# A decoder layer on one core: the order of cross-attention's products, the feed-forward's banks and the last block's transposes

## The chip, the core and the metric

The kernel runs on one core of a Trainium2 chip. A core has five engines that work side by side: TensorE (in the profile PE, its weight loads PEld), VectorE (DVE), ScalarE (ACT), GpSimd (POOL) and SyncE (SP), which here issues most of the DMAs. TensorE writes to PSUM[...]. The metric is the device time of one execution in microseconds; lower is better.

## What is computed

One layer of a decoder on 2048 tokens (32 sequences of 64) with 512 features, all in fp32. Three sublayers follow one another, each with a residual addition and a layer normalization behind it:

```python
x = layernorm(x + attention(x))                # 32 heads, 512 cached keys and 64 new ones
x = layernorm(x + cross_attention(x, context)) # 32 query heads on 8 key/value heads, 64 keys
z = x @ W.T + b                                # feed-forward
m = sum_e p[e] * (x @ A[e]) @ B[e]             # 8 terms of rank 16
gamma = minimum(0.5 * norm(z) / (norm(m) + 1e-6), 1)
x = layernorm(x + z + gamma * m)
```

## The kernel before

The tokens are cut into four blocks (`tb`) of 512, each of four tiles of 128. The large products (queries, keys and values, output projections) are computed by a scheme with seven products of half the size in each dimension in place of eight; a product is called by its number, 1 to 7, and its operands are sums that GpSimd makes ahead (`token_sums`, `output_sums`, `left_sums`, `right_sums`). One product is four matmuls of 128x128 by 256 columns. The seven are collected in three PSUM banks: x takes products 1 and 2, y takes 6, 7 and 4, z takes 5 and 3. After every product VectorE (for queries in part ScalarE) reads the bank and adds it into the result, and the next product into the same bank must wait for that read.

Self-attention fills the first two thirds of the time, and the change leaves it as it is. Then keys and values for cross-attention are computed for all groups and kept in DRAM.

**Cross-attention** runs over 32 units, one per key/value head `g` and block `tb`, `tb` innermost. The loop (lines 1274 to 1343) works on two units at once: it makes the queries and scores of unit `n` and finishes unit `n - 1`. For TensorE, VectorE and GpSimd the program's order is the order in which they run, up to unit 31, from where VectorE is ordered by the scheduler. ScalarE's and SyncE's order is the scheduler's throughout. The pieces of a turn are:

- `queries(n)` and its steps 1, 6, 5, 7, 2, 4, 3: the query products (qx in the profile), read by lines 313 to 337.
- `attend(n - 1)`: the values (pox, line 1139), eight matmuls of 64 rows, two side by side, from transposed weights `pTx` that DMAs have put in place. ScalarE (line 1157) and VectorE (line 1159) move the result to `oTx`, and GpSimd makes four sums of it (`output_sums`, lines 266 to 269).
- `scores(n)`: sx, line 1068, 32 small matmuls with 64 columns for each pair of tiles, two side by side.
- `largest`, `exponentials`, `denominators`, `weights`, `turn`: the softmax of unit `n` on VectorE and ScalarE, and its 32x32 transposes; `move(n)` issues eight DMAs from SyncE that complete the transposition into `pTx`.
- `project(n - 1, ...)`, called by `steps`: the output products (wx) of unit `n - 1`, read by lines 361 and 369.

The order before is: queries 1, 6, 5, 7, 2, 4, then pox, query 3, wx 1, sx, and wx 6, 5, 2, 7, 3, 4 with softmax parts between them. Query and wx banks and half of pox come from one pool of four banks (`xps`), the other half of pox from `xpo` (two banks), sx from `xsc` (two banks).

**Feed-forward** (lines 1193 to 1231) runs for a block at a time: block 0 at the end of unit 31's turn, block 1 between pox and the wx products of unit 31, blocks 2 and 3 after the loop. It makes pu (a rank-128 product), scales it to uT on VectorE, and for each of four tiles pz (four matmuls) and pm (one, from uT), all in banks of `xps`. VectorE adds the bias (z), ScalarE sums the squares of z and m, GpSimd adds z into the tile `acc`, VectorE computes gamma, adds gamma times m and normalizes (`layernorm_tile`, lines 174 to 184); SyncE sends the tile out. Before a block's feed-forward, `transpose_block` (x2, line 129) transposes its normalized tokens into `x1T`: four groups of transposes, each into a bank of `xps` that ScalarE or VectorE copies out (line 131). For the last block these stand between the feed-forwards of blocks 2 and 3.

Of the kernel before, what the change touches and what calls it, by code (L numbers as in the profile page):

```python
# [9 lines left out]
F32 = mybir.dt.float32  # L10
# [6 lines left out]
P = 128  # L17
# [35 lines left out]
def decoder_layer(  # L53
# [40 lines left out]
    make_identity(nc, ident)  # L94
    bk = const.tile([P, NKV], F32, name="bk")
# [23 lines left out]
    def bank(shape, name, tag=None):  # L119
        if tag in special:  # L120
            v = special[tag]
            return v.rearrange("p (a b) -> p a b", a=shape[1])
        return psum[-1].tile(shape, F32, tag=tag or "ps", name=name)
# [50 lines left out]
    def layernorm_tile(tb, j, name):  # L174
        a = acc[tb][:, j, :]
        st = small.tile([P, 6], F32, tag="st", name=f"st_{name}_{tb}_{j}")
        nc.vector.bn_stats(st, a)
        mv = small.tile([P, 2], F32, tag="mv1", name=f"mv_{name}_{tb}_{j}")
        nc.vector.bn_aggr(mv, st)
        rstd = small.tile([P, 1], F32, tag="rstd1", name=f"rstd_{name}_{tb}_{j}")  # L180
        nc.vector.tensor_scalar_add(rstd, mv[:, 1:2], LN_EPS)
        nc.scalar.activation(rstd, rstd, AF.Sqrt)
        nc.vector.reciprocal(rstd, rstd)
        nc.vector.tensor_scalar(a, a, mv[:, 0:1], rstd, ALU.subtract, ALU.mult)
# [76 lines left out]
    def output_sums(o, name):  # L261

        a = {(i, j): o[j][:, :, i * HF : (i + 1) * HF] for i in range(2) for j in range(2)}
        t = {i: big.tile([P, 2, HF], F32, tag=f"so{i}", name=f"{name}_{i}") for i in range(1, 5)}
        sub = ALU.subtract
        nc.gpsimd.tensor_tensor(t[1], a[1, 0], a[1, 1], ALU.add)  # L266
        nc.gpsimd.tensor_tensor(t[2], t[1], a[0, 0], sub)
        nc.gpsimd.tensor_tensor(t[3], a[0, 0], a[1, 0], sub)  # L268
        nc.gpsimd.tensor_tensor(t[4], a[0, 1], t[2], sub)
        return {1: a[0, 0], 2: a[0, 1], 3: t[4], 4: a[1, 1], 5: t[1], 6: t[2], 7: t[3]}  # L270
# [692 lines left out]
    with ExitStack() as ph:  # L963
# [160 lines left out]
        def attend(n):  # L1124
# [35 lines left out]
            left = output_sums(oTs.pop(n), f"sox{g}_{tb}")  # L1160
# [32 lines left out]
        def feed_forward(tb):  # L1193
            wf, af, bm = ffn_w
            pu = bank([P, TB], f"pu{tb}")
# [6 lines left out]
            for i in range(TPB):  # L1202
                u = f"{tb}_{i}"
# [3 lines left out]
                pm = bank([P, DIM], f"pm{u}")  # L1207
                for c in range(NC):
                    if c == 2:
                        nc.tensor.matmul(pm, uT[:, cols], bm, start=True, stop=True)  # L1210
                    nc.tensor.matmul(
                        pz, xT[tb][:, c, cols], wf[:, c, :], start=(c == 0), stop=(c == NC - 1)
                    )
                nrm = small.tile([P, 2], F32, tag="nrm", name=f"nrm{u}")
# [5 lines left out]
                nc.scalar.activation(sqz, z, AF.Square, accum_out=nrm[:, 0:1])  # L1220
                nc.gpsimd.tensor_tensor(a, a, z, ALU.add)
# [4 lines left out]
                nc.vector.tensor_tensor(gam, gam, nrm[:, 0:1], ALU.mult)  # L1226
                nc.vector.tensor_scalar(gam, gam, CLAMP, 1.0, ALU.mult, ALU.min)
# [35 lines left out]
        def parts(n, *made):  # L1263

            for part, pr in made:
                if n < N:
                    part(n, pr)

        def steps(n, *made):
            if n >= 0:  # L1270
                project(n, *made)

        mxs, es, dens, scales = {}, {}, {}, []
        for n in range(N + 1):
# [25 lines left out]
            if n < N:  # L1300
                q.step(4)
                q.read()
            if n > 0:
                attend(n - 1)
            if n < N:
                q.step(3)
                q.read()
                if behind:
                    next_tokens(n + 1, 0)
                next_tokens(n + 1, 1)  # L1310
            if n == N:
                feed_forward(1)
            steps(n - 1, 1)
            if n < N:
                if n + 1 < N:
                    load_kv(n + 1)
                scores(n)
            parts(n, (largest, 0), (largest, 1), (exponentials, 0), (exponentials, 1))
            if n < N and g == 0:
                for j in range(TPB):  # L1320
                    a = acc[tb][:, j, :]
                    nc.gpsimd.tensor_tensor(a, a, bo, ALU.add)
            steps(n - 1, 6)
            parts(n, (denominators, 0), (denominators, 1))
            steps(n - 1, 5)
            parts(n, (weights, 0))
            if n < N and tb == NTB - 1 and g + 1 < NKV:
                load_xq(g + 1)
            steps(n - 1, 2, 7)
            parts(n, (weights, 1))  # L1330
            steps(n - 1, 3)
            parts(n, (turn, 0), (turn, 1))
            if n < N:
                move(n)
            if n > 0:
                steps(n - 1, 4)
                if n < N and tb == 0:
                    if g > 0:
                        load_xo(g)
                    if g == NKV - 1:  # L1340
                        load_ffn()
            if n == N - 1:
                feed_forward(0)
        scales.pop(0)()
        feed_forward(2)
        while later:
            later.pop(0)()
# [50 lines left out]
```

## Time and profile before

| | us |
|---|---|
| median of 3 runs | 3067.01 (3065.17 to 3067.51) |
| the profiled execution | 3067.85 |
| its span, first to last instruction | 3066.1 |
| cross-attention, one unit in the middle | 28.51 |
| feed-forward of block 3, first to last matmul | 20.84 |
| granted TensorE clock, mean | 0.999 |

The profile is of one execution; its times differ a little from the median's. A line of the chain of waits gives the start, the length and what ran. A line of the waits reads: who waited, for whom, total us, how often, the longest. A line of the timeline is start, length, engine, line, operation, out<-in, shapes, and in brackets the idle time before it and what ended it. Matmuls overlap one another, so TensorE's pace is read from start to start.

The last stretches by engine (start:end, length, then busy time and number of instructions of PE, PEld, DVE, ACT, POOL, the granted clock, the DMA share and GB/s):

```profile
2948.57:2969.17 20.60, 20.60 (x50) 9.07 (x48) 15.04 (x41) 9.05 (x24) 3.81 (x3) 1.00 0.15 44
2969.17:2974.61 5.44, 4.32 (x33) 3.02 (x31) 5.20 (x13) 2.90 (x8) 1.27 (x1) 1.00 0.22 79
2974.61:2995.92 21.31, 20.94 (x50) 9.14 (x49) 16.18 (x40) 6.98 (x22) 8.85 (x7) 1.00 0.08 29
2995.92:3008.61 12.69, 12.35 (x57) 10.56 (x56) 11.80 (x26) 1.33 (x5) 1.27 (x1) 1.00 0.16 58
3008.61:3034.33 25.72, 22.86 (x65) 10.73 (x64) 19.51 (x50) 11.02 (x30) 5.07 (x4) 1.00 0.07 28
3034.33:3055.17 20.84, 20.84 (x48) 9.01 (x48) 14.53 (x38) 6.14 (x20) 3.80 (x3) 1.00 0.09 34
```

These are, in order: feed-forward 0; transposes of block 2 with pox of unit 31; feed-forward 1; wx of unit 31; feed-forward 2 with the transposes of block 3; feed-forward 3.

### The profile page before, as it was taken

Reading aid. Unit: us, or ns where it says so; the run is one execution under the profiler, and the core shown is the slowest. Engines: PE = TensorE matmul, PEld = TensorE weight load, DVE = VectorE, ACT = ScalarE, POOL = GpSimd, SP = SyncE. Lnnn points to the kernel's source line nnn. Section 1 sums busy time; section 2 is a strip of 40 time slices with the busy share of each in tenths; the row PEclk is TensorE's granted clock in tenths of the full one; section 3 lists DMA queues with packets and bytes.
Section 4 is the critical chain, followed back from the end, with each engine's and each line's share of the span. In section 5 each row is a group of like instructions: output and inputs, shape, how many; then the busy total and the mean of one; then the engine's idle time right before and its main releaser. Section 6 shows DMA issues by size and latency. Waiting matters only on the chain.

```text
span 3066.1 us, 42299 instructions
## 1 busy us (share of the span) xinstructions
PE 3028.1 (99%) x14944; PEld 2317.9 (76%) x14944; DVE 2171.1 (71%) x3945; ACT 766.4 (25%) x1776; POOL 961.1 (31%) x789
## 2 busy tenths in 40 slices
PE   8999999999999999999999999999999999999998
PEld 6677777777767777777777769988888888888864
DVE  7787787777877877877877764436666656666677
ACT  2323222222322233232222221211111111111232
POOL 4221321321321321322322123036434444444421
PEclk9999999999999999999999999999999999999999
DMA  5444444444344354344344343231121121121101
GB/s 173 128 132 129 109 116 128 107 122 119 104 125 118 102 130 119 101 128 120 101 125 113 91 129 141 99 108 50 55 62 52 52 66 51 51 69 49 49 28 42
DMA packets 201105, 298.66 MB, mean 97 GB/s; under 512 B 44352, under 2 KB 95040, under 8 KB 200896
## 3 DMA queue, kind: packets, MB, share of 16 engines
q1 hardware_dynamic: 186224, 280.60, 33.2%
q10 hardware_dynamic: 12624, 11.16, 1.3%
q0 software_dynamic: 2048, 4.20, 0.5%
q8 instruction: 120, 1.97, 0.3%
q14 instruction: 89, 0.73, 0.1%
HBM read 107.05 MB, written 20.97 MB: 42 GB/s over the span
## 4 chain that ended last, share of the span: by engine, by line
PE 91%; DVE 4%; SPq 2%; DMA 1%; ACT 1%; issue 1%; ACTq 0%; DVEq 0%
PE po L677 15%; PE s L631 14%; PE sx L1068 2%; PE pox L1139 2%; SPq L669 2%; PE wx_2y L292 1%; PE w_0y L292 1%; PE wx_1y L292 1%; PE wx_0y L292 1%; PE w_3y L292 1%; PE qx_3y L292 1%; PE qx_2y L292 1%; PE qx_0y L292 1%; PE q_2y L292 1%; PE wx_3y L292 1%; PE qx_1y L292 1%
## 5 line engine op out<-in xcount | busy, mean ns | idle before, releaser
L639 ACT ACTIVATE p<-s,nmax 128x576 f32<-128x576 f32 x512 | 379.1, 741 | 1244.9 <-DVE nmax L636 1234.8
L631 PE MATMUL s<-kT,qT 128*128 128x288 f32 x2048 | 576.5, 407 | 5.0 <-ACT p L639 4.2
L677 PE MATMUL po<-pT,v 128*128 128x512 f32 (+1 forms) x1280 | 549.0, 602 | 6.4 <-DMA pT<-T 6.0
L631 PEld LDWEIGHTS s<-kT,qT 128*128 128x128 f32 x2048 | 387.2, 190 | 108.0 <-issue 18.7
L636 DVE TENSOR_REDUCE nmax<-s 128x1 f32<-128x576 f32 x512 | 384.1, 750 | 59.2 <-PE s L631 59.2
L657 DVE STREAM_TRANSPOSE T<-p 128x576 f32<-128x576 f32 x512 | 394.2, 770 | 4.9 <-DVE nmax L636 0.5
L677 PEld LDWEIGHTS po<-pT,v 128*128 128x128 f32 (+1 forms) x1280 | 213.3, 189 | 206.5 <-issue 177.8
L649 DVE TENSOR_SCALAR p<-p,den 128x576 f32<-128x576 f32 x512 | 319.9, 625 | 17.9
L648 DVE RECIPROCAL den<-den 128x1 f32<-128x1 f32 x512 | 83.9, 164 | 230.0 <-ACT p L639 219.9
L266 POOL TENSOR_TENSOR so<-oT,oT 128x512 f32<-128x512 f32 x32 | 40.7, 1271 | 553.0 <-ACT oT L700 553.0
L268 POOL TENSOR_TENSOR so<-oT 128x512 f32<-128x512 f32 x32 | 40.6, 1270 | 346.2 <-ACT oT L700 95.7
L1247 POOL TENSOR_TENSOR txx<-x1T 128x512 f32<-128x512 f32 x31 | 39.3, 1267 | 229.9 <-PE qx_3z L292 93.2
L207 POOL TENSOR_TENSOR tx<-xT 128x512 f32<-128x512 f32 x31 | 39.6, 1278 | 206.3 <-PE q_3z L292 65.0
L639 ACT ACTIVATION_READ_ACCUMULATOR p<-s,nmax 128x1 f32 x512 | 98.7, 193 | 0.0
L266 POOL TENSOR_TENSOR sox<-oTx,oTx 128x512 f32<-128x512 f32 x32 | 40.5, 1265 | 181.5 <-DVE oTx L1159 176.0
L1085 ACT ACTIVATE ex<-ex 128x512 f32<-128x512 f32 x64 | 39.3, 630 | 203.2 <-DVE ex L1084 203.2
L1068 PEld LDWEIGHTS sx<-kvx,qTx 128*64 128x64 f32 x2048 | 62.3, 138 | 10.6 <-issue 10.6
L700 ACT COPY oT<-po 128x512 f32<-128x512 f32 x128 | 68.2, 587 | 4.7 <-PE po L677 3.8
L1157 ACT ACTIVATE oTx<-pox,bv 128x256 f32<-128x256 f32 x128 | 52.0, 470 | 66.4 <-PE pox L1139 66.4
L1068 PE MATMUL sx<-kvx,qTx 128*64 128x64 f32 x2048 | 66.7, 224 | 0.0
L1139 PE MATMUL pox<-pTx,kvx 64*128 64x256 f32 x512 | 64.6, 389 | 0.0
L1159 DVE TENSOR_SCALAR oTx<-pox,bv 128x256 f32<-128x256 f32 x128 | 53.6, 479 | 9.9 <-PE pox L1139 9.9
(447 smaller groups left out, 5767.6 us busy)
## 6 DMA issues: line engine op xcount, KB each, us to landing
pT<-T SPq DMA_DIRECT2D x1016, 80.0 KB
pT<-T SPq DMA_DIRECT2D x1008, 64.0 KB
xT<-in_xT SPq DMA_DIRECT2D x31, 1024.0 KB
kvx<-kv SPq DMA_DIRECT2D x32, 512.0 KB
pTx<-Tx SPq DMA_DIRECT2D x256, 64.0 KB
kv<-c SPq DMA_DIRECT2D x30, 512.0 KB
wo<-in_woT SPq DMA_DIRECT2D x32, 256.0 KB
xwq<-in_xwq SPq DMA_DIRECT2D x32, 256.0 KB
```

The source lines that it names most:

```text
L266: nc.gpsimd.tensor_tensor(t[1], a[1, 0], a[1, 1], ALU.add)
L292: nc.tensor.matmul(self.banks[b][:, m, :], self.left[i][:, k, m * P : (m + 1) * P], self.right[i][:, k, :], start=(first and m + k == 0), ...
L631: nc.tensor.matmul(s[:, a, :HALF], qTs[n // REP][:, units[n][2], i * P : (i + 1) * P], kTs[g][:, a * HALF : (a + 1) * HALF], start=True, s ...
L636: nc.vector.tensor_reduce(nmax, s[:, :, :HALF], AX.XY, ALU.max, negate=True)
L639: nc.scalar.activation(p.rearrange("q (a k) -> q a k", a=2), s[:, :, :HALF], AF.Exp, bias=nmax, accum_out=den,)
L648: nc.vector.reciprocal(den, den)
L649: nc.vector.tensor_scalar(p, p, den, None, ALU.mult)
L657: nc.vector.transpose(Ts[n][:, :, i, :], ps_.pop((n, i)).rearrange("q (b k) -> q b k", k=SQ))
L677: nc.tensor.matmul(pos[n].rearrange("d (a q) -> d a q", a=NQD), vs[units[n][0]][rows, v, :], pTs[n // 2][rows, :, chunk, :], skip_group_ch ...
L700: nc.scalar.copy(o[:, i, :].rearrange("d (t a k) -> d a t k", t=TPB, a=NQD), pos.pop(n - 1 + i).rearrange("d (a t k) -> d a t k", a=NQD, t ...
L1068: nc.tensor.matmul(s[b * SEQ : (b + 1) * SEQ, i * REP + h, :], qTs[n][:, h, pr * HF + c0 : pr * HF + c0 + SEQ], kvs[n][:, pr, 0, c0 : c0 + ...
L1139: nc.tensor.matmul(po[pr, b][:, i, :].rearrange("d (h a j) -> d h a j", h=REP, a=2), kvs[n][r, pr, 1, i * HD : (i + 1) * HD], pTs[n][r, :, ...
```

## The change

It has four parts.

1. In a turn of the cross-attention loop all seven query products come first, then pox, sx, and wx in the order 1, 5, 6, 3, 7, 2, 4. The softmax parts are spread among them anew, `turn` and `move` come after wx 4, and GpSimd makes the third and fourth of its sums in the other order, following the order of use.
2. The feed-forward takes pu from the score banks and, from block 1 on, pm from the two banks `po0` and `po1`. In a block's first tile pm comes after pz's four matmuls; in the others after the second, as before.
3. VectorE, not GpSimd, adds z into `acc`. The factor 0.5 of gamma moves into ScalarE's square, so gamma takes three small VectorE instructions in place of four. The epsilon of the layer normalization is given to ScalarE's root as a bias from a constant tile that GpSimd sets at the start, in place of an addition on VectorE.
4. The last block's transposes come ahead of the fourth tile of block 2's feed-forward, in place of behind it.

```diff
+    eps = const.tile([P, 1], F32, name="eps")
+    nc.gpsimd.memset(eps, LN_EPS)
...
-        nc.vector.tensor_scalar_add(rstd, mv[:, 1:2], LN_EPS)
-        nc.scalar.activation(rstd, rstd, AF.Sqrt)
+        nc.scalar.activation(rstd, mv[:, 1:2], AF.Sqrt, bias=eps)
...
-    def output_sums(o, name):
+    def output_sums(o, name, fourth_last=True):
...
-        nc.gpsimd.tensor_tensor(t[3], a[0, 0], a[1, 0], sub)
+        if fourth_last:
+            nc.gpsimd.tensor_tensor(t[3], a[0, 0], a[1, 0], sub)
         nc.gpsimd.tensor_tensor(t[4], a[0, 1], t[2], sub)
+        if not fourth_last:
+            nc.gpsimd.tensor_tensor(t[3], a[0, 0], a[1, 0], sub)
...
-        def feed_forward(tb):
+        def feed_forward(tb, between=None):
             wf, af, bm = ffn_w
-            pu = bank([P, TB], f"pu{tb}")
+            pu = sc.tile([P, TB], F32, tag="sc", name=f"pu{tb}")
...
             for i in range(TPB):
+                if between and i == TPB - 1:
+                    between()
...
-                pm = bank([P, DIM], f"pm{u}")
+                pm = (pp.tile([P, DIM], F32, tag=f"po{i % 2}", name=f"pm{u}") if tb else
+                      bank([P, DIM], f"pm{u}"))
                 for c in range(NC):
-                    if c == 2:
-                        nc.tensor.matmul(pm, uT[:, cols], bm, start=True, stop=True)
                     nc.tensor.matmul(
                         pz, xT[tb][:, c, cols], wf[:, c, :], start=(c == 0), stop=(c == NC - 1)
                     )
+                    if c == (NC - 1 if i == 0 else 1):
+                        nc.tensor.matmul(pm, uT[:, cols], bm, start=True, stop=True)
...
-                nc.scalar.activation(sqz, z, AF.Square, accum_out=nrm[:, 0:1])
-                nc.gpsimd.tensor_tensor(a, a, z, ALU.add)
+                nc.scalar.activation(sqz, z, AF.Square, scale=CLAMP, accum_out=nrm[:, 0:1])
+                nc.vector.tensor_tensor(a, a, z, ALU.add)
...
-                nc.vector.tensor_tensor(gam, gam, nrm[:, 0:1], ALU.mult)
-                nc.vector.tensor_scalar(gam, gam, CLAMP, 1.0, ALU.mult, ALU.min)
+                nc.vector.tensor_scalar(gam, gam, nrm[:, 0:1], 1.0, ALU.mult, ALU.min)
...
             if n < N:
                 q.step(4)
                 q.read()
+                q.step(3)
+                q.read()
             if n > 0:
                 attend(n - 1)
             if n < N:
-                q.step(3)
-                q.read()
+                if n + 1 < N:
+                    load_kv(n + 1)
+                scores(n)
                 if behind:
                     next_tokens(n + 1, 0)
                 next_tokens(n + 1, 1)
             if n == N:
                 feed_forward(1)
-            steps(n - 1, 1)
-            if n < N:
-                if n + 1 < N:
-                    load_kv(n + 1)
-                scores(n)
-            parts(n, (largest, 0), (largest, 1), (exponentials, 0), (exponentials, 1))
+            parts(n, (largest, 0), (largest, 1))
...
+            steps(n - 1, 1, 5)
+            parts(n, (exponentials, 0))
             steps(n - 1, 6)
-            parts(n, (denominators, 0), (denominators, 1))
-            steps(n - 1, 5)
-            parts(n, (weights, 0))
+            parts(n, (exponentials, 1), (denominators, 0))
+            steps(n - 1, 3)
+            parts(n, (denominators, 1))
             if n < N and tb == NTB - 1 and g + 1 < NKV:
                 load_xq(g + 1)
-            steps(n - 1, 2, 7)
+            steps(n - 1, 7)
+            parts(n, (weights, 0))
+            steps(n - 1, 2)
             parts(n, (weights, 1))
-            steps(n - 1, 3)
-            parts(n, (turn, 0), (turn, 1))
-            if n < N:
-                move(n)
             if n > 0:
                 steps(n - 1, 4)
+                parts(n, (turn, 0), (turn, 1))
+                if n < N:
+                    move(n)
...
         scales.pop(0)()
-        feed_forward(2)
-        while later:
-            later.pop(0)()
+        feed_forward(2, later.pop(0))
         feed_forward(3)
```

More of the change, by code (lines that the diff above doesn't have):

```diff
@@ L1159, in attend @@
                             nc.vector.tensor_scalar(dst, src, bias, None, ALU.add)
-            left = output_sums(oTs.pop(n), f"sox{g}_{tb}")
+            left = output_sums(oTs.pop(n), f"sox{g}_{tb}", False)
             pjs[n] = Projection(left, wo_cur[g], tb, f"wx{g}_{tb}", XYZ)
@@ L1341, in decoder_layer @@
                         load_ffn()
+            if n == 0:
+                parts(n, (turn, 0), (turn, 1))
+                move(n)
             if n == N - 1:
```

## The prediction

> **What bounds the kernel now.** I read the page first, then the chain of waits inside one cross-attention unit, then what TensorE waited for, then the stretches of the end and the two engines beside it.
>
> ```profile
> PE 3028.1 (99%) x14944; PEld 2317.9 (76%) x14944; DVE 2171.1 (71%) x3945; ACT 766.4 (25%) x1776; POOL 961.1 (31%) x789
> ```
>
> TensorE is busy 99% of the span, and between 2100 and 2890 us the list of its waits is empty. So the change can only give time where TensorE's own work gets shorter, or at the end of the kernel, where it does wait. The chain in the middle of a unit (start, length, what) shows the first:
>
> ```profile
> 2407.88 1.73 PE qx_1x L292 x8
> 2409.61 1.73 PE qx_1y L292 x8
> 2411.33 1.93 PE pox L1139 x16
> 2413.26 1.92 PE qx_1z L292 x8
> 2415.18 1.73 PE wx_0x L292 x8
> 2416.91 2.02 PE sx L1068 x64
> 2418.93 1.92 PE wx_0y L292 x8
> 2420.85 1.73 PE wx_0z L292 x8
> ```
>
> A product of eight matmul records takes 1.73, but 1.92 directly after pox (64-row tiles) or sx (64-column tiles): 0.19 for coming back to the full array. A unit is 12 x 1.73 + 2 x 1.92 + 1.93 + 2.02 = 28.5. TensorE's waits from 2890 us on:
>
> ```profile
> PE x L129 <- ACT x1T L131: 2.2, 2, 1.1
> PE pu L1197 <- DVE gam L1224: 1.8, 1, 1.8
> PE x L129 <- ACT qTx L328: 1.0, 2, 0.5
> PE x L129 <- DVE x1T L131: 0.6, 2, 0.3
> PE pm L1210 <- DVE uT L1201: 0.4, 1, 0.4
> ```
>
> And what paces VectorE there (timeline, feed-forward of the last block):
>
> ```profile
> 3047.54 1.58 DVE L184 TENSOR_SCALAR acc<-acc,mv_f,rstd_f 128x512 f32<-128x512 f32 x1
> 3047.58 1.26 POOL L1221 TENSOR_TENSOR acc<-acc,z 128x512 f32<-128x512 f32 x1 [3.14 <-DVE rstd_f L183]
> 3062.07 0.55 DVE L184 TENSOR_SCALAR acc<-acc,mv_f,rstd_f 128x512 f32<-128x512 f32 x1
> ```
>
> The same normalization takes 1.58 beside GpSimd's addition and 0.55 alone. The chain shows gam L1224 starting at 3044.11, 3049.13, 3054.05 and 3058.97: VectorE needs 4.92 a tile, TensorE 4.29 (pz L1211 after pz). After TensorE's last matmul (3055.2) another 11 us pass.
>
> [...]
>
> **The change, part by part.** Sums are against the profiled execution: span 3066.1, whole 3067.85 (1.75 around it).
>
> *Pox directly ahead of sx.* The third query product no longer follows pox, so it takes 1.73: 0.19 less per unit. Pox still follows a full-array product (1.93). Sx now follows pox, one entry as before (2.02); the trace has no pox-to-sx pair, so this entry could cost 0.1 less or up to 0.19 more; I take the same, since each is one change of shape. W1 then follows sx (1.92). Units 1 to 31: 31 x 0.19 = **-5.9**.
>
> Does a wait take its place? Put P at the start of pox in the new order: sx at P+1.9, w1 at 3.9, w5 5.8, w6 7.5, w3 9.2, w7 11.0, w2 12.7, w4 14.4.
> - *GpSimd's sums*: before, they start at P+3.1 and need 1.27 each, so t1, t2, t4, t3 are there at 4.4, 5.7, 6.9, 8.2; used at 5.8, 7.5, 9.2, 11.0. More slack than before, where w6 stood at 7.6.
> - *Banks*: products into one bank now stand closer (w5-w3, w6-w7 with one product between), so VectorE must have read the first in 1.7 us. VectorE in its written order: two q3 additions to 1.0, evictions 1.3 to 2.95, both maxima to 4.7, w1's two reads (0.68 and 1.22) 6.0 to 7.8, w5's read to 8.5 (needed at 9.2), exponentials, w6's read to 10.1 (needed 11.0), second exponentials, denominators, w3's read to 12.0, denominators, w7's read to 13.5 (needed 14.4). Slack 0.7 to 0.9.
> - *Transposes and pT*: turn ends at P+18.3, before at 18.4. The eight issues take 4.95 and their packets land about 1.4 later, at P+24.7; the next pox is at P+28.3. In seven units the first quarter of the next group's query weights is now issued ahead of these DMAs and waits for the next unit's first product (P+18.1), plus up to 1.4 for its own issue (5.46 for four): slack falls from 3.6 to about 2.3. Key loads and weights keep their place relative to P; the output weights' last quarter comes 1.9 earlier, and GpSimd's sums queue behind it with at least 5 us over.
>
> All of it is cover, so nothing is added. The first unit is special: pox(0) took 2.36 instead of 1.93, waiting for pT; one product later it finds it landed: **-0.4**. The 1.55 wait for L333 at 2063 stays.
>
> *Head.* The added memset of eps stands on GpSimd before the iota chain (0.1); VectorE waits for the block indices until 3.24 while the iota result is used by 2.27: hidden, 0.
>
> *VectorE's tile in the feed-forward.* Removed: adding eps to the variance (0.2), one gam instruction (0.2), the slow normalization (1.58 to 0.55). Added: z's addition, two SBUF inputs, which the trace does not have in this place; the nearest rows are 0.68 (L1218) and 0.69 (L1094), so a pitch of 0.60 when another instruction follows; between 0.55 and 1.3. ScalarE's root now has nothing of VectorE beside it, 0.45 from aggregate to reciprocal. Sum of pitches: z 0.60, normalization 0.46, addition 0.60, gam 0.65, L1228 0.79, statistics 0.73, aggregate and root 0.45, reciprocal 0.17, some 0.05 of waiting for ScalarE = 4.5. So VectorE remains the slower of the two, at 4.5 against 4.29 (before 4.92).
> - *Last block* from its pu: the first gam comes at the same place (9.7 after pu: now pm last, before z last). Then 2.8 to the next z, two tiles of 4.5, and 5.1 for the last: 16.9, before 3062.62 - 3044.11 = 18.5. **-1.7** with rounding.
> - *Block 0 to block 1*: before, block 0's last z is read 22.0 after its pu; after, 9.7 + 2.8 + 2 x 4.5 = 21.5. That read and the first copy hold the third and fourth transposes (stretch 2969.17 to 2974.61): 0.6 less. Placing pm last in the first tile removes block 1's wait for uT: 0.37 and 0.1 of restart, as behind every stop. **-1.2** with rounding. The wait of 0.34 in the last output products goes, but w3 there waits for VectorE's read of w5, about as long: 0.
>
> *Last transposes ahead of tile 3.* Before: feed-forward 2 takes from 3008.61 to 3029.21 on TensorE, then 5.12 until pu of block 3 (2.14 of transposes, 2.98 of waits: a bank, a bank, copies). After: the transposes stand after tile 2, at 16.3 from its pu. The fourth needs the bank of tile 2's z, which VectorE reads by 17.7, and stands at 17.9. Tile 3's z bank needs the first copy, done by 17.7, needed at 18.4. The copies (0.58 to 0.64 each) delay gam of tile 2 by about 1.2 on VectorE, which tile 3's 4.29 covers. pu of block 3 has a score bank and starts at 22.7, before 25.72: **-3.0**, between -2 (a second wait for a bank) and -3.
>
> Sum: 5.9 + 0.4 + 1.7 + 1.2 + 3.0 = 12.2. 3067.85 - 12.2 = 3055.65 for the profiled execution, which lies 0.84 above the median: **3054.8**.
>
> **Rivals.**
> - *A shape change between two tiled modes costs as much as two.* Then the 5.9 go: 3067.0 - 6.3 = 3060.7. For: no such pair in the trace. [...]
> - *The end gives half.* The addition on VectorE costs 1 us, or the copies make tile 3 late, and the last three terms give 2.9 instead of 5.9: 3057.8. For: VectorE has no slack there. Against: nothing contends any more.
> - *Slower: VectorE late in the output products.* One place: w3 waiting for w5's read, w7 for w6's. It decides when VectorE runs over 0.7 us later than worked out; above 1.1 us late (0.4 x 31 = 12.2) the whole is slower. At 1.4 us: 31 x 0.7 = 21.7 - 12.2 = +9.5, 3076.5. For: it is busy 17.7 of a unit's 28.5 us, and only one product lies between where two or more lay. Against: each of its steps comes from a measured row, and its two-input additions that GpSimd slows (L1094, 0.69 to 1.47) stand behind the reads that decide.
>
> **How the numbers follow.** Forecast 0.68, half the end 0.12, no saving from shapes 0.12, VectorE late 0.08. The range holds the forecast with its open costs (3051 to 3058) and the two faster rivals: 3051 to 3061. About 0.2% (6.1 us) is what a measurement of this kernel can tell from no change; the shape rival lies on that border and is split. Faster 0.84, same 0.08, slower 0.08.
>
> **What would show it.** In the changed profile's chain a unit of 28.3 instead of 28.5, the third query product at 1.73, sx at about 2.0 directly after pox, and no TensorE wait between 2100 and 2880. In the end: L184 at 0.55 everywhere, gam of the last block every 4.5, no wait of pu of block 3. Wrong would be waits of wx z or y for VectorE's L361, sx above 2.2, or pu waiting for copies.

## The result, and the profile after

| | before | after |
|---|---|---|
| median, us | 3067.28 (3065.17 to 3069.44, 6 runs) | 3056.09 (3054.30 to 3057.02, 6 runs) |
| ratio, 95% interval | | 0.9962 (0.9952 to 0.9973) |
| the profiled execution | 3067.85 | 3057.02 |
| its span | 3066.1 | 3055.2 |
| first query product of cross-attention to pu of block 0 | 906.49 | 903.34 |
| pu of block 0 to the end | 117.50 | 109.70 |

The kernel is 11.2 us faster; 3054.8 was forecast. The sum is near, but by luck, for it is made of other parts: the cross-attention loop gave 3.1 instead of 6.3, and the end gave 7.8 instead of 5.9. Distances in a trace are taken here from the first query product of cross-attention, since the start of that product differs from one execution to the next (2039.2 to 2044.8 in the thirteen further traces of this study) for kernels that are the same up to there but for the one memset of eps.

The engines' line of the page after the change shows TensorE at 99%, as before:

```profile
PE 3021.4 (99%) x14944; PEld 2320.5 (76%) x14944; DVE 2171.4 (71%) x3929; ACT 768.5 (25%) x1776; POOL 944.8 (31%) x774
```

The chain of waits inside the same unit (start, length, what):

```profile
2410.10 1.73 PE qx_1z L296 x8
2411.83 1.93 PE pox L1143 x16
2413.75 2.02 PE sx L1072 x64
2415.77 1.92 PE wx_0x L296 x8
```

The third query product takes 1.73, pox 1.93 and sx 2.02: sx costs directly behind pox what it cost behind a product. One product of 1.92 is left. A unit is 28.31 instead of 28.51, in every undisturbed unit. TensorE's waits from 2100 us on:

```profile
PE x L131 <- ACT qTx L332: 1.5, 2, 1.0
PE qx_2y L296 <- DVE rstd_x L165: 1.2, 1, 1.2
PE qx_0y L296 <- POOL xwq L203: 1.2, 1, 1.2
...
PE x L131 <- DVE z L1227: 0.4, 1, 0.4
```

The stops of the end (x1T of ScalarE, pu on gam, pm on uT) are gone (one of 0.6 on x1T of VectorE, as before, is left out here); the 0.4 on z is what is left of the stop at block 2's transposes. But the second and third line are new, and the first was 1.0 before. These three are what the loop did not give, and they go against the forecast's sign "no TensorE wait between 2100 and 2880". The first in time stands at the entry of unit 4, the first unit of group 1 (timeline of GpSimd and TensorE):

```profile
2136.66 4.96 POOL L1330 TENSOR_TENSOR acc<-acc,bo 128x512 f32<-128x512 f32 x4
2141.58 1.72 POOL L201 TENSOR_TENSOR xwq<-xwq,xwq 128x512 f32<-128x512 f32 x1
...
2145.06 1.27 POOL L203 TENSOR_TENSOR xwq<-xwq,xwq 128x512 f32<-128x512 f32 x1
2146.38 1.99 PE L296 MATMUL qx_0y<-txx,xwq 128*128 128x256 f32 x8 [1.18 <-POOL xwq L203]
```

In group 0 alone GpSimd also adds the output bias, four additions that stand ahead of the sums of the next group's query weights. Product 6 needs the third of these sums. Before the change it was done 0.75 us ahead of that product; now pox and all that follows it on GpSimd come one product later, and it is ready 1.2 us too late. The second stands at the entry of unit 30, in the last group, where output product 4 brings the layer norm's statistics with it (timeline of VectorE and TensorE):

```profile
2881.71 0.69 DVE L151 BATCH_NORM_STATS2 st_x<-acc 128x6 f32<-128x512 f32 x1
...
2885.40 1.30 DVE L1108 STREAM_TRANSPOSE Tx<-ex 128x512 f32<-128x512 f32 x2 [0.20 <-issue]
2886.63 0.65 DVE L337 TENSOR_TENSOR qTx<-qx_2y,qTx 128x512 f32<-128x512 f32 x1
2887.43 1.96 PE L296 MATMUL qx_2y<-txx,xwq 128*128 128x256 f32 x8 [1.19 <-DVE rstd_x L165]
```

Statistics and turn keep VectorE from 2881.71 to 2886.63, and only then it reads query product 6, which product 7 waits for, as it goes to the same bank. (The list names rstd_x, the small instruction behind the read.) The third is in unit 31:

```profile
2920.23 2.93 ACT L169 ACTIVATE acc<-acc,shift_x,rstd_x 128x512 f32<-128x512 f32 x4 [1.56 <-DVE shift_x L167]
2923.07 0.81 ACT L332 ACTIVATE qTx<-qx_3x,bq 128x256 f32<-128x256 f32 x2
2923.93 1.12 PE L131 MATMUL x<-ident,acc 128*128 128x128 f32 x8 [1.03 <-ACT qTx L332]
```

ScalarE's scaling follows the statistics, its read of query product 2 follows the scaling, and the transposes wait for the bank of that product. Against the rest of the loop these three cost 1.45, 1.43 and 0.54 us, measured from start to start.

The stretches that answer to those shown of before (transposes with pox, feed-forward 1, wx of unit 31, feed-forward 2 with transposes; feed-forward 0 and 3, with 20.60 and 20.76, are nearly as they were):

```profile
2966.15:2970.50 4.35, 3.96 (x33) 3.11 (x32) 3.92 (x11) 3.00 (x8) 0.00 (x0) 1.00 0.18 63
2970.50:2991.20 20.70, 20.70 (x50) 9.23 (x49) 15.34 (x38) 7.24 (x23) 5.15 (x4) 1.00 0.10 38
2991.20:3003.37 12.17, 12.17 (x57) 10.56 (x56) 10.21 (x22) 1.52 (x5) 0.00 (x0) 1.00 0.12 45
3003.37:3025.72 22.35, 22.35 (x65) 10.82 (x64) 16.52 (x44) 10.30 (x27) 0.00 (x0) 1.00 0.06 24
```

TensorE now is idle only in the first of them. VectorE's tile in the last block (timeline):

```profile
3039.68 0.15 DVE L1233 TENSOR_SCALAR gam<-nrm 128x1 f32<-128x1 f32 x1
3043.04 0.54 DVE L185 TENSOR_SCALAR acc<-acc,mv_f,rstd_f 128x512 f32<-128x512 f32 x1
3044.15 0.15 DVE L1233 TENSOR_SCALAR gam<-nrm 128x1 f32<-128x1 f32 x1
```

The normalization takes 0.54 to 0.55 in all sixteen tiles, and in this block gam comes every 4.47 us.

### The profile page after: what moved, and what is told of

Its sections match the earlier page's. It is cut to its first block, busy times and chain, and to the rows that moved or that the text cites. A ratio compares the mean times of both kernels' runs of the same rounds, so it can differ in the third digit from the quotient of the medians.

```text
span 3055.2 us, 42257 instructions
## 1 busy us (share of the span) xinstructions
PE 3021.4 (99%) x14944; PEld 2320.5 (76%) x14944; DVE 2171.4 (71%) x3929; ACT 768.5 (25%) x1776; POOL 944.8 (31%) x774
## 4 chain that ended last, share of the span: by engine, by line
PE 93%; DVE 3%; DMA 1%; SPq 1%; ACT 1%; issue 1%; POOL 0%; ACTq 0%; DVEq 0%; POOLq 0%
PE po L681 16%; PE s L635 15%; PE sx L1072 2%; PE pox L1143 2%; PE w_2y L296 1%; PE q_3y L296 1%; PE w_0y L296 1%; PE w_3y L296 1%; PE qx_0y L296 1%; PE wx_1y L296 1%; PE wx_0y L296 1%; PE wx_3y L296 1%; PE q_2y L296 1%; PE qx_2y L296 1%; PE qx_1y L296 1%; PE qx_3y L296 1%
```

## The experiments

"Trace" is the distance from the first query product of cross-attention to the end of the span; "against after" is the difference in it to the changed kernel. A ratio is to executions of the kernel before that were measured beside the run.

| run | median (runs) | ratio to before, 95% | trace | against after |
|---|---|---|---|---|
| before | 3067.28 (6) | | 1023.99 | +10.95 |
| after | 3056.09 (6) | 0.9962 (0.9952 to 0.9973) | 1013.04 | |
| E1 loop alone | 3065.13 (13) | 0.9992 (0.9983 to 1.0000) | 1024.28 | +11.24 |
| E2 end alone | 3058.77 (7) | 0.9973 (0.9962 to 0.9984) | 1016.44 | +3.40 |
| E3 bias additions late | 3054.43 (5) | 0.9958 (0.9945 to 0.9972) | 1011.56 | -1.48 |
| E4 turn first | 3056.89 (7) | 0.9968 (0.9957 to 0.9979) | 1014.99 | +1.95 |
| E5 additions, statistics and transposes late | 3050.50 (5) | 0.9944 (0.9931 to 0.9958) | 1007.08 | -5.96 |
| E6 pox and sx apart | 3062.22 (20) | 0.9985 (0.9978 to 0.9991) | 1018.91 | +5.87 |
| E7 z on GpSimd | 3057.92 (6) | 0.9968 (0.9956 to 0.9980) | 1014.37 | +1.33 |
| E8 transposes behind the fourth tile | 3059.05 (9) | 0.9973 (0.9963 to 0.9983) | 1015.11 | +2.07 |
| E9 banks back | 3057.10 (6) | 0.9966 (0.9954 to 0.9978) | 1013.93 | +0.89 |
| E10 transposes late | 3051.94 (5) | 0.9950 (0.9936 to 0.9964) | 1009.93 | -3.11 |
| E11 statistics split | 3056.84 (5) | 0.9966 (0.9952 to 0.9980) | 1016.29 | +3.25 |
| E12 arithmetic back | 3060.09 (13) | 0.9978 (0.9969 to 0.9986) | 1017.45 | +4.41 |

The intervals of the ratios are about 0.2% wide, so single medians do not separate differences of one or two us; the traces do, as long as the granted clock is the same. It was not in E1, E4 and E11, whose last column is too high for that reason.

### E1 and E2: the two halves alone

E1 puts only the new loop (diff part 1) into the kernel before, E2 only the rest.

> The kernel before with the first part of the change alone: the new order of cross-attention's unit and the output sums with the fourth one last. The feed-forward, its banks, the normalisation's epsilon and the last block's transposes are as before. Theory 1 (the order saves 0.198 us in each of 31 units and 0.4 in the first, and gives back 3.4 in three waits inside the loop: 1.45 at the entry of unit 4 on the query weights' sums, 1.43 at the entry of unit 30 behind the statistics, 0.54 in unit 31): the time falls by about 3.0 us, and the list of TensorE's waits has qx_0y on xwq with about 1.2 and qx_2y on rstd_x with about 1.2. Rival 2 (the waits of the last group come from the feed-forward's new banks and issue places, which reach into the last units; the order alone is clean): the time falls by 5.0 to 6.5 us, and qx_2y on rstd_x is not in the list.

> The kernel before with everything but the first part: feed-forward in the attention's banks, z added by VectorE, epsilon in the activation, the last block's transposes ahead of tile 3 of block 2; the order of cross-attention's unit is the old one. Theory 1 (the end's gain of 7.8 us arises behind the last unit and does not lean on the new order): the time falls by about 7.8 us (7.2 to 8.2), with no new wait of TensorE in the loop. Rival 2 (part of the end's gain is an effect of the order, for example product 2 as the last but one of the output products, which removes a wait on bank x): the time falls by 5.5 to 7.0 us only, and the sum of both parts alone falls short of the whole.

E1 reached pu of block 0 at 903.34, as the changed kernel did, 3.15 us earlier than before, with the same three waits. So these belong to the order, not to the feed-forward's banks. But then this execution, 3.8 us above E1's median, lost all of it again. Two of the lines of its waits:

```profile
PE pu L1200 <- DVE gam L1227: 1.8, 1, 1.8
PE wx_3z L295 <- DVE gam L1230: 1.2, 1, 1.2
```

The second is new: in the new order the last unit's output products come to a bank that VectorE, at the pace of the old arithmetic, frees late, and 0.9 us go (E12, with the old arithmetic, has this wait too; E9, with the old banks, has not). The first was there before too, but in this execution the granted clock fell to 0.50 within that stop, at 3031.74, for 6.83 us (stretches: the stop, and pu of block 3; the last three numbers are the granted clock, the DMA share and GB/s):

```profile
3031.01:3032.78 1.77, 0.01 (x1) 0.03 (x1) 1.74 (x5) 0.30 (x2) 0.15 (x1) 0.71 0.27 101
3032.78:3039.32 6.54, 6.54 (x9) 2.84 (x10) 2.92 (x9) 0.20 (x1) 0.00 (x0) 0.56 0.14 53
```

From pu's start to that of pz it took 6.38 us, in the kernel before 3.51. Without that the trace would have shown a gain of some 2.6 us (an estimate), which agrees with the medians (2.4, with an interval that reaches down to no gain). E2 gave 7.55 in the trace and had no new wait in the loop, so rival 2's 5.5 to 7.0 fell. Its last clause came true in the traces: both halves together give 10.95, about 0.8 more than the 2.6 and 7.55 of the halves, since the end's new arithmetic removes the wait on wx_3z that the order brings. By the medians the halves add up to the whole (2.4 + 8.8 and 11.2), but these cannot tell 0.8.

### E3: the bias additions behind the weights' sums

```diff
-            if n < N and g == 0:
+            if n < N and g == 0 and tb < NTB - 1:
                 for j in range(TPB):
...
                 load_xq(g + 1)
+            if n < N and g == 0 and tb == NTB - 1:
+                for j in range(TPB):
+                    a = acc[tb][:, j, :]
+                    nc.gpsimd.tensor_tensor(a, a, bo, ALU.add)
```

> The changed kernel with one edit: in the last unit of group 0 GpSimd makes the sums of the next group's query weights ahead of the four additions of the output bias (4.96 us) and not behind them. Theory 1 (these additions hold the sums back, and query product 6 of unit 4 waits 1.18 us for them): the wait of qx_0y on xwq is gone, the start of every later unit is 1.2 to 1.45 us earlier, and the time is 1.2 to 1.5 us under the changed kernel's. Rival 2 (the weights' sums wait for the DMA of the weights or for product 3 of unit 3, not for GpSimd): the sums start where they did, at most 0.3 us earlier, and nothing is gained.

Timeline of GpSimd:

```profile
2135.78 1.27 POOL L201 TENSOR_TENSOR xwq<-xwq,xwq 128x512 f32<-128x512 f32 x1
2141.05 5.87 POOL L1342 TENSOR_TENSOR acc<-acc,bo 128x512 f32<-128x512 f32 x4
```

The sums start 5 us earlier against unit 4's products and wait for nothing; the list of TensorE's waits between 2100 and 2885 is empty, and everything from unit 4 on is 1.45 earlier. Theory 1 holds.

### E4: turn ahead of output product 4 in the last group

```diff
-                steps(n - 1, 4)
+                last = units[n - 1][0] == NKV - 1
+                if not last:
+                    steps(n - 1, 4)
                 parts(n, (turn, 0), (turn, 1))
                 if n < N:
                     move(n)
+                if last:
+                    steps(n - 1, 4)
```

> The changed kernel with one edit: in the last group the turn and its DMAs stand ahead of output product 4's read and the statistics that hang on it, as in the kernel before; everything else of the new order stays. Theory 1 (VectorE has no gap there: turn 1.24 us and statistics 3.6 us fill it from the weights to the read of query product 6 in either order, and the softmax stands about 1 us nearer to the next unit's products than before; only the gap of 0.3 us ahead of output product 4's read is won): qx_2y still waits, 0.7 to 1.0 us instead of 1.19, and the time is 0.2 to 0.8 us under the changed kernel's. Rival 2 (the turn behind the statistics is the whole cause): the wait of qx_2y is gone and that of the transposes on qTx is back at 1.0 in total, and the time is 1.7 to 2.0 us under the changed kernel's.

```profile
PE x L131 <- ACT qTx L332: 2.7, 2, 2.2
PE qx_2y L296 <- DVE rstd_x L165: 0.6, 1, 0.6
```

The list of TensorE's waits shows the wait of unit 30 halved, to 0.6 where theory 1 had 0.7 to 1.0, but in unit 31 the scaling came later and the transposes stopped 2.18 us, just behind which the granted clock was 0.50 for 3.41 us. In sum the trace is 1.95 us longer, the greater part of it by the clock (an estimate: 3.41 us at half the clock are 1.7 us of work); the median is 0.8 higher. The order of the turn was not the whole cause (rival 2 fell), and the time of theory 1 was missed: it left out the scaling.

### E5: bias additions, statistics and transposes moved

Beside E3's edit: of the statistics behind units 28 and 29 two tiles come behind the turn and two behind the read of query product 6, the scaling behind query product 2, the transposes ahead of pox. The diff shows the moves, without E3's and without the split of the statistics into two calls.

```diff
                     if stat and i == 6:
-                        scales.pop(0)()
+                        stat.pop(0)(range(2, TPB))
...
-            while later:
-                later.pop(0)()
             if n < N:
                 q.step(4)
...
                 q.step(3)
                 q.read()
+            while later:
+                later.pop(0)()
```

> The changed kernel with the bias additions of the last unit of group 0 behind the weights' sums, as in the run before, and for the layer norms behind units 28 and 29: two tiles' statistics behind the turn, two behind the read of query product 6, the scaling on ScalarE behind query product 2's reads, and the four transposes of a block directly ahead of the attend piece (behind query product 3). Theory 1 (the two losses of the last group are the statistics on VectorE, which keep the read of query product 6, and the scaling on ScalarE, which keeps query product 2's read and so the bank of the transposes): the waits of qx_2y on rstd_x (1.2) and of x on qTx (1.5 in two) are gone or under 0.3 each, and the time is 1.5 to 2.7 us under that of the run with the bias additions alone, near 3052. Rival 2 (moving the statistics only moves the stop: the maxima and exponentials or the evictions of attend come late instead, and output products or the next attend wait): new waits of 1 us and more behind sx in units 29 to 31, and the time is within 0.5 us of the run with the bias additions alone.

All three waits are gone; of the list from 2100 us on one line remains, the 0.4 for z. A unit with transposes takes 30.06 us, both times: 28.31 and 1.75. It was 32.77 and 31.88 after the change and 31.54 twice before it. The gain over E3 is 4.48 in the trace, more than either theory had: theory 1 counted idle times, 2.7 in all, while from start to start the two units stood 2.7 and 1.8 above 30.06. It is the fastest of all versions, 0.9944 of before (0.9931 to 0.9958) where the changed kernel has 0.9962.

### E10 and E11: which of E5's moves gives it

E10 makes only the second half of the diff above: the transposes behind query product 3. E11 splits the statistics as in E5 and leaves scaling and transposes where they were.

> The changed kernel with one edit: the four transposes of each block of the layer norm stand behind query product 3, directly ahead of attend, and not behind query product 2. Statistics and scaling stay where they were. Theory 1 (where they stood they wait for ScalarE's read of query product 2, which stands behind the scaling of four tiles; between product 2 and attend two products give it 3.45 us): the stops of x on qTx (1.5) and on x1T (0.6) are gone, a unit with transposes costs 1.75 us more than one without instead of 3.0 to 3.5, and the time is 2.5 to 3.4 us under the changed kernel's; the wait of qx_2y on rstd_x (1.2) stays. Rival 2 (the statistics are what delays all of it): the transposes still wait, and at most 1 us is gained.

> The changed kernel with one edit: of the statistics behind units 28 and 29 two tiles stand behind the turn and two behind the read of query product 6; the scaling follows as before, and the transposes stay behind query product 2. Theory 1 (only the wait of query product 7 on the read of product 6 goes; the scaling is not earlier against the products, so the transposes wait as long or longer): the wait of qx_2y on rstd_x is gone, that of x on qTx is 1.5 to 3.5 in two, and the time is between 1.2 us under and 0.8 over the changed kernel's. Rival 2 (the statistics are the cause of both losses): both waits go, and the time is 2.0 to 2.7 us under.

E10, timeline of TensorE in unit 30:

```profile
2891.44 1.89 PE L296 MATMUL qx_2z<-x1T,xwq 128*128 128x256 f32 x8
2893.16 1.91 PE L131 MATMUL x<-ident,acc 128*128 128x128 f32 x16
```

All sixteen transposes run in one piece. In E11 the wait of product 7 is gone, but the transposes stop longer, and the clock falls to 0.50:

```profile
2895.28 3.02 PE L131 MATMUL x<-ident,acc 128*128 128x128 f32 x12 [2.18 <-ACT qTx L334]
2898.08 3.62 PE L298 MATMUL qx_2y<-txx,xwq 128*128 128x256 f32 x8
```

Both first theories hold in their waits, and both rivals fell. E10's gain is 3.11 and E3's 1.48; the remaining 1.37 of E5's 5.96 is about what the wait of product 7 cost (1.43). E11 does not win it, since the longer stop of the transposes takes it back. E11's profiled execution, with the lower clock, lies 6.0 us above its median, and the median within 1 us of the changed kernel's.

### E6: pox and sx apart again

```diff
-                q.step(3)
-                q.read()
             if n > 0:
                 attend(n - 1)
             if n < N:
+                q.step(3)
+                q.read()
+            steps(n - 1, 1)
+            if n < N:
...
-            steps(n - 1, 1, 5)
+            steps(n - 1, 5)
```

> The changed kernel with cross-attention's TensorE order of before between the products: query product 4, attend, query product 3, output product 1, scores. Attend and scores no longer touch; VectorE's order of the reads stays close to the changed kernel's. Theory 1 (a change between the full array and the smaller tiles and back costs 0.198 us, and the change saves one of two per unit): the period of an undisturbed unit is 28.51 instead of 28.31, 31 x 0.198 = 6.1 us more; the wait of 1.2 us at the entry of unit 4 goes or shrinks, since attend and with it the output sums are 1.7 us earlier against the query products; the time is 4.0 to 6.2 us over the changed kernel's. Rival 2 (the gain per unit is that of the new order of VectorE's and GpSimd's work, not of the two touching pieces): the period stays at 28.31 to 28.40 and the time is 0 to 2.5 us over.

Chain of waits in a unit:

```profile
2409.77 1.93 PE pox L1143 x16
2411.70 1.92 PE qx_1z L296 x8
2413.62 1.73 PE wx_0x L296 x8
2415.35 2.02 PE sx L1072 x64
2417.36 1.92 PE wx_0z L296 x8
```

There are two products of 1.92 and a period of 28.51, with VectorE's and GpSimd's new order kept but for the moved pieces: the 0.198 per unit is the way back to the full array, and rival 2 fell. The wait of unit 4 is gone here, since pox and the sums behind it stand 1.7 earlier; that of unit 30 is not, and wx_3x waits 0.8 for oTx in the last unit, which is new. The wait that went (1.45 less), the new one (0.8 more), 6.1 in the units and 0.4 in the first unit make up the 5.87.

### E7, E9, E12 and E8: the end

E7 gives z's addition back to GpSimd. E12 gives back all of the feed-forward's arithmetic: besides z also epsilon on VectorE and gamma in four instructions. E9 takes pu and pm from the old pool; E8 has the transposes behind the fourth tile.

In E7 and E12:

```diff
-                nc.vector.tensor_tensor(a, a, z, ALU.add)
+                nc.gpsimd.tensor_tensor(a, a, z, ALU.add)
```

In E12 also:

```diff
-        nc.scalar.activation(rstd, mv[:, 1:2], AF.Sqrt, bias=eps)
+        nc.vector.tensor_scalar_add(rstd, mv[:, 1:2], LN_EPS)
+        nc.scalar.activation(rstd, rstd, AF.Sqrt)
...
-                nc.vector.tensor_scalar(gam, gam, nrm[:, 0:1], 1.0, ALU.mult, ALU.min)
+                nc.vector.tensor_tensor(gam, gam, nrm[:, 0:1], ALU.mult)
+                nc.vector.tensor_scalar(gam, gam, CLAMP, 1.0, ALU.mult, ALU.min)
```

In E9:

```diff
-            pu = sc.tile([P, TB], F32, tag="sc", name=f"pu{tb}")
+            pu = bank([P, TB], f"pu{tb}")
...
-                pm = (pp.tile([P, DIM], F32, tag=f"po{i % 2}", name=f"pm{u}") if tb else
-                      bank([P, DIM], f"pm{u}"))
+                pm = bank([P, DIM], f"pm{u}")
```

In E8:

```diff
-        feed_forward(2, later.pop(0))
+        feed_forward(2)
+        while later:
+            later.pop(0)()
```

> The changed kernel with one edit: the addition of z to the residual is GpSimd's again. Theory 1 (a GpSimd addition beside it stretches the normalisation on VectorE from 0.54 to about 1.5 us, while z's addition on VectorE costs 0.6): VectorE's tile in the last block takes 4.85 to 4.95 instead of 4.47 us, the normalisation's mean is 1.3 to 1.5 us, and the time is 1.2 to 2.2 us over the changed kernel's. Rival 2 (GpSimd takes 1.27 us and ends before VectorE gets to the normalisation, or the tile is set by TensorE): the tile stays within 0.1 of 4.47, the time within 0.4 us.

> The changed kernel with the feed-forward's products of pu and pm in the output products' banks again; the place of the pm product, z on VectorE, epsilon and the transposes' place stay. Theory 1 (the banks carry part of the end's gain: with them the stops of block 0 to 1 and the last unit's output products go; in the run of the order alone wx_3z waited 1.2 us for the first read of a bank by VectorE's gam chain): pu of block 1 starts 0.7 to 1.1 us later against pu of block 0, pu of block 2 another 0.5 to 1.2 us, and the time is 1.2 to 2.8 us over the changed kernel's. Rival 2 (with z on VectorE and the transposes ahead, the path of the end runs through VectorE, and the banks are always read in time): 0 to 0.5 us over.

> The changed kernel with the feed-forward's arithmetic of before: z added by GpSimd, epsilon added by VectorE ahead of the root, and gam in four instructions; banks, the place of the pm product and the last transposes' place stay new. In the run with z alone on GpSimd the normalisation kept its 0.54 us, because VectorE's order there has the reciprocal ahead of z, so that the normalisation starts 0.23 us before GpSimd's addition. With the old arithmetic the order has z ahead of the reciprocal, as in the kernel before, and both engines start within 0.05 us of each other. Theory 1 (it is which of the two starts first that decides who is stretched, and the epsilon and gam edits, not z's move, freed the normalisation): the normalisation's mean is 1.2 to 1.4 us again, VectorE's tile in the last block 4.85 to 4.95 us against 4.60 with z alone and 4.47 in the changed kernel, and the time is 2.3 to 4.0 us over the changed kernel's. Rival 2 (the banks or the pm product's place took the stretch away): the normalisation stays at 0.54 to 0.65 us, the tile at 4.6 to 4.75, and the time is 1.3 to 2.2 us over.

> The changed kernel with one edit: the last block's transposes stand behind the fourth tile of block 2 again. Theory 1 (pu of block 3 then waits for VectorE's copies behind the fourth tile, a stop of TensorE of 2.9 us in two pieces, with nothing else to do): pu of block 3 starts 2.8 to 3.4 us later against pu of block 2, and the time is 2.8 to 3.4 us over the changed kernel's; if the granted clock falls behind that stop, as it did in one run here (0.50 to 0.57 over 6 us, 2.9 us lost), up to 6.3. Rival 2 (the last block is bound by VectorE's tiles, whose first can start no earlier than VectorE has done block 2's last): at most 0.8 us over.

| us in the trace | before | after | E7 | E12 | E9 | E8 |
|---|---|---|---|---|---|---|
| pu of block 0 to pu of block 1 | 26.04 | 24.96 | 25.27 | 26.01 | 24.94 | 24.95 |
| to pu of block 2 | 34.00 | 32.87 | 33.26 | 34.14 | 32.87 | 32.88 |
| to pu of block 3 | 25.72 | 22.35 | 22.51 | 22.68 | 23.26 | 24.34 |
| to the end | 31.74 | 29.52 | 29.99 | 31.28 | 29.52 | 29.61 |

The columns of E7 and E12 tell what was not expected. E7, timeline of one tile of the last block:

```profile
3044.24 0.54 DVE L185 TENSOR_SCALAR acc<-acc,mv_f,rstd_f 128x512 f32<-128x512 f32 x1
3044.47 1.44 POOL L1230 TENSOR_TENSOR acc<-acc,z 128x512 f32<-128x512 f32 x1 [3.17 <-DVE z L1227]
```

and E12:

```profile
3044.05 1.59 DVE L186 TENSOR_SCALAR acc<-acc,mv_f,rstd_f 128x512 f32<-128x512 f32 x1
3044.09 1.27 POOL L1231 TENSOR_TENSOR acc<-acc,z 128x512 f32<-128x512 f32 x1 [3.66 <-DVE rstd_f L185]
```

With z alone on GpSimd the normalization is not stretched (0.54 to 0.55 in 15 of 16 tiles, and gam every 4.60 us); GpSimd's addition is, 1.44 instead of 1.27. With epsilon on ScalarE and gamma in three instructions, VectorE's order has the reciprocal ahead of z, and the normalization starts directly behind z, 0.23 before GpSimd. With the old arithmetic z stands ahead of the reciprocal, both start within 0.04, and it is the normalization that is stretched: its mean is 1.30, and gam comes every 4.92 us. Theory 1 of E7 fell in its reason, though its time came; theory 1 of E12 holds for the normalization and the tile, and its time is at or above the upper end (4.0 by the medians, 4.4 us in the trace), as the waits of x on x1T and of wx_3z, 1.1 each, came back with it. The recorded starts alone do not tell which of the two is stretched: in E12's fence VectorE starts 0.04 ahead and takes 1.59, and in tiles of the earlier blocks of the kernel before, with the same arithmetic, GpSimd starts 0.02 to 0.03 ahead and the normalization takes 1.52 to 1.53 (at 2961.61 and 2961.64, for one). What decides between these tiles and E7's, where VectorE leads by 0.23, is not shown beyond that. The 1.59 is 1.05 more than the 0.54 of E7's tile.

E9: the banks are worth 0.9 us, all of it between blocks 2 and 3, where the transposes ahead of the fourth tile then stop for banks (timeline of TensorE):

```profile
3021.56 1.06 PE L131 MATMUL x<-ident,acc 128*128 128x128 f32 x8 [0.21 <-ACT x1T L133]
3022.86 1.99 PE L1217 MATMUL pz<-wf,x1T 128*128 128x512 f32 x4 [0.24 <-ACT x1T L133]
```

Neither of its theories named that place or size. E8 is worth 2.0 us in the same stretch, less than the 2.8 to 3.4 of theory 1: with the new banks and arithmetic the stop ahead of pu is one of 1.69, no longer two of 2.87 together. The medians give 2.9 to 3.0. The profiled execution lies 3.0 us under E8's median; what the others lost is not shown.

## Why the prediction was right in sum and wrong in parts

- *Pox directly ahead of sx, 31 x 0.19 = 5.9.* Right: 0.198 a unit, 6.1 in 31 units, and in the place named, the product behind pox. Sx behind pox is 2.02; the rival of a doubled entry fell. E6 shows it by undoing it. The first unit's 0.4 came too (0.43).
- *"All of it is cover, so nothing is added."* This step failed. It was worked out for a unit in the middle, where it holds: VectorE's reads were in time, and the rival of late reads fell. It was not worked out for units that carry extra work. The forecast gave GpSimd's sums behind the output weights "at least 5 us over", but did not work out the sums of the query weights, ahead of which 4.96 us of bias additions stand in group 0; and it left out that output product 4 brings 3.5 us of statistics with it in the last group. Together 3.4 us were lost in three places. E3 shows the first; E4, E10 and E11 show that in the last group the statistics delay product 7 and the scaling delays the transposes.
- *VectorE's tile, 4.92 to 4.5.* The number was right (4.47), its reason was not. The forecast freed the normalization by taking z from GpSimd. E7 and E12 show that z's move gives 0.13 a tile, and that epsilon's and gamma's edits together give 0.32. In E12 the stretched normalization puts 1.52 between its start and gam; in E7 this is 1.17, of which VectorE idles 0.63 for ScalarE's root, so the 1.05 of stretch costs the tile only about a third of itself. That the place of the reciprocal is the cause is read from the timelines; epsilon and gamma were not put back one by one.
- *Block 0 to block 1, 1.2; last output products, 0.* Of the 1.2, the 0.6 for the transposes was 1.08. The rest, uT's stop, falls behind pu of block 1: 0.61 (21.31 to 20.70) instead of 0.5, since this stop, with 0.37 idle, costs more from start to start than its idle time, as unit 4's does (1.18 idle, 1.45 from start to start). The last output products gave 0.52 (12.69 to 12.17) instead of 0, as the wait of wx_3x went without another in its place. E12 shows the first and the last to be the arithmetic's: with it back the first stretch is 26.01 as before, and the last output products take 13.44 with the wait of wx_3z. That E12's second stretch, 34.14, is near that of before is chance. Feed-forward 1 stays at 20.70 in E12 and in E9, so neither the arithmetic nor the banks alone took uT's stop away; what is left is the place of pm, which no run undoes alone.
- *Last transposes ahead of tile 3, 3.0.* It was 3.37: the transposes ran in one piece, 1.75 us long, without the expected stop for a bank. Put back alone, the place costs 2.0 in this stretch (E8), the banks 0.9 (E9), the arithmetic 0.3 (E12).
- *Last block, 1.7.* It was 2.2: 1.86 between TensorE's last matmul and VectorE's last end, by the tile; 0.28 in the landing of the last output, and 0.08 on TensorE. The landing is not the change's: from VectorE's last end to the end it is 3.46 before and 3.19 after, but 3.49 in E2 with the new end and 3.19 in E1 with the old one.

So a term of 6.3 gave 3.1 and terms of 5.9 gave 7.8. The two errors arise in different places and nearly cancel: that the sum came within 1.3 us is luck. The rivals all fell: the saving from the shapes came, the end gave more and not half, and VectorE was in time in the output products.

## What to carry to other kernels

When a period of a loop gets shorter, work out the waits again for the iterations that carry more than the others: the first group, the last group, the one that loads weights. There the cover ends first. A moved instruction is to be judged by what starts beside it, not only by its own length: two small instructions on VectorE, epsilon's addition of 0.15 us and one of gamma's, decided here, with z on GpSimd, whether the normalization took 0.54 or up to 1.59 us. And work that waits for a late engine, like the transposes here, is best put where a product or two still lie between: E10 gained as much by one move as the whole rewritten loop did (3.1 us each in the traces).

## What the runs showed of the hardware

- The clock granted to TensorE fell to 0.50 in or just behind stops of 2.18 us (for 3.41 us in E4, 6.83 in E11) and in the second of two stops of 1.10 and 1.77 us (6.83 us in E1). It stayed at 1.00 behind the like stops of 1.11 and 1.76 in the kernel before, so the length of a stop alone does not decide; what else does is not shown. In E1 the fall cost some 2.9 us (6.38 instead of 3.51 from pu's start to that of pz) behind stops of 2.87 together, as much again as the stops themselves.
- A change from the 64-row tiles of pox to the 64-column tiles of sx costs no more than one from the full array (sx takes 2.02 either way), and a way back to the full array costs 0.19 to 0.20 us.
- VectorE's normalization and GpSimd's addition do not slow each other evenly: 0.54 and 1.44 when VectorE leads by 0.23 us, 1.59 and 1.27 when the recorded starts lie within 0.04.
